# Handing out two small PSUM tiles in the order in which they come free

## The chip, the cores and the metric

The kernel runs on one core of a Trainium2 chip. The metric is the device time of one execution in microseconds (us): the median of several runs, lower is better. Before the change it was 32416.63 us, the median of 3 runs from 32408.93 to 32426.16.

## What is computed

Eight images of 56 x 56 pixels with 192 channels go through four layers, all in float32. Layer 0 sends half of the channels through three convolutions and the other half through a normalisation, a projection, a depthwise convolution and a selective scan in four directions; layers 1 and 2 are selective scans in four directions with a layer norm behind them; layer 3 is windowed attention (7 x 7 windows, shifted by 3, six heads) with an MLP. The scan is the bulk of the work:

```
def step(h, t):
    u_t, d_t, b_t, c_t = t
    h = jnp.exp(d_t[..., None] * A) * h + (d_t * u_t)[..., None] * b_t[:, :, None, :]
    return (h, jnp.einsum('bkdn,bkn->bkd', h, c_t))
...
delta = jax.nn.softplus(jnp.einsum('bkrl,kdr->bkdl', dts, dt_proj_w) + dt_proj_b[None, :, :, None])
...
yv = _ln(yv, out_norm_g, out_norm_b) * jax.nn.silu(z)
```

Here `h` has 16 states for each of 192 channels, `t` runs over 3136 pixels in each of four directions, and layer 0's norm works over the 192 channels of a pixel.

## The kernel before

**The scan steps.** `run` (line 766) walks 9216 steps: 8 images, three scan layers, four directions, four chunks of 784 pixels (`CK`), and within a chunk 24 steps of 128 rows (32 channels x 4 states). In each step ACT makes `exp(delta*A)` into a large PSUM tile `ps_x`, POOL makes `db` (delta*u times B), DVE runs the scan over 784 pixels, and DVE (three steps of four) or POOL (the fourth) multiplies by C into a buffer `hc`. Every third step PE adds up three `hc` buffers into the PSUM tile `ps_y` (`add_up`, line 992), and ACT copies the finished sums out (`merge`, line 1013). There are seven `hc` buffers, three `db` buffers and two `ps_x` tiles.

**Everything else is woven between the steps by hand.** Python generators record the other work: `prepare` (line 921: the softplus that makes delta for the next half chunk), `after` and `after_half` (lines 658 and 677: the norm behind each scan layer, and the projection to the next layer's B, C and dt), `ssm_front` and `conv_front` (layer 0's front and convolutions of the next image), and `attention_block` (line 1029: layer 3 of the image before). `run` lets the generators in three queues (`ahead`, `urgent`, `back`) advance piece by piece after each step. A `yield n` gives the turn back, for `n` steps if `n` is over 0. `together(2, ...)` (line 380) advances two generators in turn. The order in which the generators record their instructions is then the order on each engine: `in_order` (line 881) ties every instruction to the one recorded before it on its engine. What happens when on the chip is decided by these five queues and by semaphore waits.

**The small PSUM tiles.** Two tiles of 128 x 512 float32, called `ps_p`, serve all work outside the scan steps. A generator asks with `bank()` (line 351), which calls `all_banks(1)` (line 356). It yields until the count of free tiles, `self.banks`, is at least 1 and no queue of higher rank has asked in the last step. Then the count goes down and a tile is taken from the pool `self.psum` with tag `p` and two buffers: the pool gives its two buffers in turn. `free()` (line 365) puts the count up again. It is called when the last reader of the tile has been recorded, not when that reader has run. The pool adds the wait of the new user's first instruction for all that the previous user of the same buffer does.

**The users that matter below.** `ln_cm` (line 401) takes a tile, records two matmuls into it (the sums of the 192 channels, by a matrix of ones), two DVE instructions that subtract the mean (`act<-ps_p,act`), and frees it, without a yield between; then `to_norm` (line 413) takes a tile for the variance (`aux,ones`). `after` runs two halves of `after_half` in `together(2, ...)`. `softplus` (line 940) holds a tile from its matmul (`ps_p<-dts,dtw`) to its last DVE subtraction (`spe<-ps_p,spe`), over several yields; its two halves also run two at a time. The attention takes tiles for the query and key sums (`xb,wqkv`), their squared norms (`qksq,blk`), the scores (`biasl,ident` and `kn,qn`), the values (`wqkv,xw`), the transposed scores (`ident,s`), the weighted sums (`vt,pt`, read by DVE into `o`), and the transposed result (`ident,o`).

Matmuls are float32 and run as two passes each, transposes as one, so the profile shows more PE rows than the program has matmuls. Nearly all instructions pass through one helper that counts their load, so that their line in the profile is L109; they are told apart by the names of their tiles.

Of the kernel before, what the change touches and what calls it, by code (L numbers as in the profile page):

```python
# [31 lines left out]
F32 = mybir.dt.float32  # L32
# [6 lines left out]
C = 192  # L39
CH = 96  # L40
T = 448
# [7 lines left out]
HC = CK // 2  # L49
# [89 lines left out]
class Net:  # L139
    def __init__(self, ctx, tc, a, out):  # L140
        self.tc, self.nc, self.a, self.out = tc, tc.nc, a, out
        self.cp = ctx.enter_context(tc.tile_pool(name="const", bufs=1))
        self.dram = ctx.enter_context(tc.tile_pool(name="dram", bufs=1, space=bass.MemoryType.DRAM))
        self.dram2 = ctx.enter_context(
            tc.tile_pool(name="dram2", bufs=2, space=bass.MemoryType.DRAM)
        )
        self.psum = ctx.enter_context(tc.tile_pool(name="psum", bufs=2, space=bass.MemoryType.PSUM))
        self.psum1 = ctx.enter_context(tc.tile_pool(name="psum1", bufs=1, space=bass.MemoryType.PSUM))
        self.constants(ctx)
        self.wout = self.const("wout", [CH, 2, C])  # L150
        big = ctx.enter_context(tc.tile_pool(name="big", bufs=1))
        self.bufs = [big.tile([CH, 2, L], F32, name=f"act{n}") for n in range(2)]
        for n in (1, 2, 3, 4, 5):
            setattr(self, f"s{n}", ctx.enter_context(tc.tile_pool(name=f"s{n}", bufs=n)))
        self.s6 = ctx.enter_context(tc.tile_pool(name="s6", bufs=HCS))
        self.ranks = self.s1.tile([CH, CK], F32, name="dts")
        self.aux = [self.s1.tile([CH, 2, HC], F32, name=f"aux{n}") for n in range(2)]
        self.nc.gpsimd.memset(self.ranks, 1.0)
        self.done = set()
        self.nc = Engines(tc.nc)  # L160
        self.load = self.nc.load
        self.now, self.banks, self.rank, self.asked = 0, 2, 0, [-9] * 3
        self.ahead, self.urgent, self.back = deque(), deque(), deque()
        self.u0, self.sz, self.xl, self.u3, self.bcd = {}, {}, {}, {}, {}

    def ps(self, tag, p=128, n=512):
        if tag == "y":
            t = self.psum1.tile([128, 1024], F32, name="ps_y")
        else:
            w = 512 if tag == "p" else 1024  # L170
            t = self.psum.tile([128, w], F32, name=f"ps_{tag}", tag=tag)
        return t[:p, :n]
# [183 lines left out]
    def all_banks(self, n):  # L356
        rank = self.rank
        while self.banks < n or any(at >= self.now - 1 for at in self.asked[rank + 1 :]):
            self.asked[rank] = self.now
            yield 1  # L360
        self.asked[rank] = -9
        self.banks -= n
        return [self.psum.tile([128, 512], F32, name="ps_p", tag="p") for _ in range(n)]

    def free(self):

        self.banks += 1
# [33 lines left out]
    def ln_cm(self, x, n, sq):  # L401

        nc = self.nc
        p = (yield from self.bank())[:CH, :n]
        for c in range(2):
            nc.tensor.matmul(p, self.ones, x[:, c, :], start=c == 0, stop=c == 1)
        for c in range(2):
            nc.vector.scalar_tensor_tensor(x[:, c, :], p, -1.0 / C, x[:, c, :], ALU.mult, ALU.add)
        self.free()
        yield 1  # L410
        yield from self.to_norm(x, n, sq)

    def to_norm(self, x, n, sq):

        nc = self.nc
        nc.scalar.activation(sq, x, AF.Square)
        yield 1
        p = (yield from self.bank())[:CH, :n]
        for c in range(2):
            nc.tensor.matmul(p, self.ones, sq[:, c, :], start=c == 0, stop=c == 1)  # L420
        yield LAG
        nc.scalar.activation(p, p, AF.Ln, bias=self.eps[:CH], scale=1.0 / C)
        nc.scalar.activation(p, p, AF.Exp, scale=-0.5)
        yield 0
        for c in range(2):
            nc.vector.tensor_mul(x[:, c, :], p, x[:, c, :])
        self.free()
        yield 1
# [41 lines left out]
    def ssm_front(self, b):  # L470
# [3 lines left out]
        with tc.tile_pool(name="f1", bufs=1) as f1, tc.tile_pool(name="f2", bufs=2) as f2:  # L474
# [14 lines left out]
            def depthwise(r, c, u):  # L489
                p = (yield from self.bank())[:CH, :T]  # L490
                for tap in range(9):
                    dy, dx = tap // 3, tap % 3
                    nc.tensor.matmul(
                        p, diag[:, c, tap, :], pads[r % 3][:, c, dy : dy + ROWS, dx : dx + HW],
                        start=tap == 0, stop=tap == 8,
                    )
                    if tap % 3 == 2:
                        yield 1
                yield 1
                nc.scalar.activation(u[:, c, :], p, AF.Identity, bias=self.v("conv2d_b", c))  # L500
                self.free()
                yield 1

            def gate(xnt, r, e, sz):
                p = (yield from self.bank())[:CH, :T]
                nc.tensor.matmul(p, win[:, CH * e : CH * e + CH], xnt, start=True, stop=True)
                yield LAG
                if e < 2:
                    self.band(
                        [t[:, e] for t in pads], r,  # L510
                        lambda dst, rows: nc.scalar.copy(dst, grid(p)[:, rows, :]),
                    )
                else:
                    nc.scalar.copy(sz[:, e - 2, :], p)
                self.free()
                yield 1

            for r in range(NR + 1):
                sz = u = None
                if r < NR:  # L520
# [18 lines left out]
                    p = (yield from self.bank())[:CH, :T]  # L539
# [7 lines left out]
                    self.free()  # L547
# [17 lines left out]
    def conv_front(self, b):  # L565
# [3 lines left out]
        with tc.tile_pool(name="f1", bufs=1) as f1, tc.tile_pool(name="f2", bufs=2) as f2:  # L569
# [6 lines left out]
            def conv(w, pads, r):  # L576
                p = (yield from self.bank())[:CH, :T]
                for tap in range(9):
                    dy, dx = tap // 3, tap % 3
                    nc.tensor.matmul(  # L580
                        p, w[:, tap, :], pads[r % 3][:, dy : dy + ROWS, dx : dx + HW],
                        start=tap == 0, stop=tap == 8,
                    )
                    if tap % 3 == 2:
                        yield 1
                yield 1
                return p

            def first(r):
                tok = self.tokens(f2, b, r, "tokl", 0, CH)  # L590
                yield 2
                p = (yield from self.bank())[:CH, :T]
# [9 lines left out]
                self.free()  # L602
                yield 1

            def second(r):
                p = yield from conv(wc1, pad1, r)
# [5 lines left out]
                self.free()  # L612
                yield 1

            def third(r):
                p = yield from conv(wc2, pad2, r)
# [4 lines left out]
                self.free()  # L621
# [4 lines left out]
                def last(c):  # L626
                    p = (yield from self.bank())[:CH, :T]
# [3 lines left out]
                    self.free()  # L631
                    yield 1
                    p = (yield from self.bank())[:CH, :T]
# [7 lines left out]
                    self.free()  # L641
# [35 lines left out]
    def after_half(self, g, q):  # L677
# [22 lines left out]
        if l == 0:  # L700
# [6 lines left out]
            ps = [p[:CH, :HC] for p in (yield from self.all_banks(2))]  # L707
            for c in range(2):
                for j in range(2):
                    nc.tensor.matmul(  # L710
                        ps[c], self.wout[:, j, CH * c : CH * c + CH], y[:, j, :],
                        start=j == 0, stop=j == 1,
                    )
            yield LAG
            for c in range(2):
                nc.vector.tensor_add(y[:, c, :], ps[c], aux[:, c, :])
                self.free()
            yield 1

    def project(self, g, par, i):  # L720
# [7 lines left out]
        for q in range(2 * i, 2 * i + 2):  # L728
            p = (yield from self.bank())[:W, :HC]
# [8 lines left out]
            self.free()  # L738
# [182 lines left out]
    def prepare(self, U, h, start):  # L921
# [18 lines left out]
        def softplus(q):  # L940
            p = (yield from self.bank())[:CH, :HC]
# [17 lines left out]
            self.free()  # L959
# [99 lines left out]
    def attention(self, x, wi, bias, wqkv, wpr, q1, q2):  # L1059
# [15 lines left out]
        def normed(c, j, name):  # L1075
            p = (yield from self.bank())[:CH, :BT]
# [6 lines left out]
            self.free()  # L1083
# [3 lines left out]
            p = (yield from self.bank())[:CH, :BT]  # L1087
# [7 lines left out]
            if j:  # L1095
                nc.vector.tensor_mul(kn[:, c, :], p, t)
                self.free()
            else:
                nc.vector.tensor_mul(t, p, t)
                self.free()  # L1100
# [12 lines left out]
        def pair(w0):  # L1113
# [4 lines left out]
            for d in range(2):  # L1118
                w = w0 + d
                p = (yield from self.bank())[:WT, : HEADS * WT]  # L1120
# [21 lines left out]
                self.free()  # L1142
                yield 0
            p = (yield from self.bank())[:WT, : 2 * C].rearrange("n (d e) -> n d e", d=2)
# [11 lines left out]
            self.free()  # L1156
            pts = q2.tile([WT, 2, HEADS * WT], F32, name="pt")
            for d in range(2):
                p = (yield from self.bank())[:WT, : HEADS * WT]
# [6 lines left out]
                self.free()  # L1166
                yield 0
            yield 1
            p = (yield from self.bank())[:WT, : 2 * C].rearrange("n (d e) -> n d e", d=2)
# [12 lines left out]
            self.free()  # L1182
            yield 1
            p = (yield from self.bank())[:CH, : 4 * WT]
# [17 lines left out]
            self.free()  # L1202
# [5 lines left out]
        def project(c):  # L1208
            p = (yield from self.bank())[:CH, :BT]
# [8 lines left out]
            self.free()  # L1218
# [18 lines left out]
    def mlp(self, x, wi, b, f1b, wf1, q1, q2):  # L1237
# [5 lines left out]
        def expand(m):  # L1243
            p = (yield from self.bank())[:, :BT]
# [7 lines left out]
            self.free()  # L1252
# [9 lines left out]
        for c in range(2):  # L1262
            p = (yield from self.bank())[:CH, :BT]
# [8 lines left out]
            self.free()  # L1272
# [4 lines left out]
        def store(a):  # L1277
            n = min(2, WS - a) * HW
            p = (yield from self.bank())[:n, :C]
# [7 lines left out]
            self.free()  # L1287
# [143 lines left out]
```

## Time and profile before

| | |
|---|---|
| median of 3 runs | 32416.63 us |
| lowest and highest run | 32408.93 and 32426.16 us |
| the profiled execution, its own time | 32427.15 us |
| its span, first to last instruction | 32425.0 us |
| mean granted TensorE clock | 0.697 of full speed |
| DVE waits for PE work on `ps_p` before `o` | 467.2 us in 198 waits |
| DVE waits for POOL's `db` before a scan into `ps_x` | 757.9 us in 666 waits |
| DVE waits for POOL's `db` before a scan into `hc` | 39.7 us in 49 waits |
| DVE waits for PE work on `ps_y` before `hc` | 257.5 us in 124 waits |

PE is TensorE, PEld its weight loads, DVE VectorE, ACT ScalarE, POOL GpSimd, SP the engine that issues most DMAs. A group's row in the profile gives, after the shapes and the count, the busy time in us and the mean ns of one instruction, then the idle time of the engine just before the group's instructions and what ended most of it. The stretches of work repeat from layer to layer and image to image: over the 40 equal slices of the span DVE is 70 to 90% busy nearly throughout.

### The profile page before, as it was taken

Reading aid. Unit: us, or ns where it says so; the run is one execution under the profiler, and the core shown is the slowest. Engines: PE = TensorE matmul, PEld = TensorE weight load, DVE = VectorE, ACT = ScalarE, POOL = GpSimd, SP = SyncE. Lnnn points to the kernel's source line nnn. Section 1 sums busy time; section 2 is a strip of 40 time slices with the busy share of each in tenths; the row PEclk is TensorE's granted clock in tenths of the full one; section 3 lists DMA queues with packets and bytes.
Section 4 is the critical chain, followed back from the end, with each engine's and each line's share of the span. In section 5 each row is a group of like instructions: output and inputs, shape, how many; then the busy total and the mean of one; then the engine's idle time right before and its main releaser. Section 6 shows DMA issues by size and latency. Waiting matters only on the chain. (4 is left out here: it accounts for less than half of the span.)

```text
span 32425.0 us, 276524 instructions
## 1 busy us (share of the span) xinstructions
PE 20473.4 (63%) x77812; PEld 7417.8 (23%) x77812; DVE 25991.6 (80%) x22723; ACT 18456.6 (57%) x38862; POOL 24426.9 (75%) x14431
## 2 busy tenths in 40 slices
PE   4665466666666666666666666666666666666556
PEld 1221122222222222222222222222212222222123
DVE  2889887888888888888888888788887888888870
ACT  2555555565556655566555655556555665655553
POOL 2888877778777787778777787777877778777860
PEclk8776667667776777666776767767777667666666
DMA  2455544445444454444544455444544445444430
GB/s 57 116 124 115 115 113 106 111 103 124 111 108 104 109 126 109 108 105 113 121 105 111 106 117 117 107 107 108 118 116 106 107 108 120 108 110 106 110 88 13
DMA packets 1538509, 3473.09 MB, mean 107 GB/s; under 512 B 345563, under 2 KB 538164, under 8 KB 1536965
## 3 DMA queue, kind: packets, MB, share of 16 engines
q1 hardware_dynamic: 1533700, 3455.30, 46.3%
q8 instruction: 615, 10.08, 0.1%
q14 instruction: 930, 7.61, 0.1%
q10 hardware_dynamic: 2496, 0.09, 0.0%
q0 software_dynamic: 768, 0.01, 0.0%
HBM read 1457.23 MB, written 147.89 MB: 50 GB/s over the span
## 5 line engine op out<-in xcount | busy, mean ns | idle before, releaser
L109 POOL TENSOR_TENSOR db<-usp,bt 128x784 f32<-128x784 f32 x9216 | 16857.4, 1853 | 2672.5 <-DVE ps_x L109 1431.6
L109 DVE TENSOR_TENSOR_SCAN ps_x<-ps_x,state,db 128x784 f32<-128x784 f32 x5184 | 9563.7, 1845 | 1175.8 <-POOL db L109 565.4
L109 ACT ACTIVATE ps_x<-dsp,A 128x784 f32<-128x784 f32 x9216 | 8433.7, 916 | 2676.7 <-DVE hc L109 2476.5
L109 PE MATMUL ps_y<-hc,esum 128*32 128x392 f32 x36864 | 7205.9, 668 | 1598.6 <-POOL hc L109 1416.2
L109 DVE TENSOR_TENSOR hc<-ps_x,ct 128x784 f32<-128x784 f32 x6912 | 6738.8, 975 | 718.3 <-PE ps_y L109 106.4
L109 POOL TENSOR_TENSOR hc<-hc,ct 128x784 f32<-128x784 f32 x2304 | 4249.8, 1845 | 2876.2 <-ACT state L109 2370.9
L109 ACT COPY state<-ps_x 128x1 f32<-128x1 f32 x5184 | 812.8, 157 | 5513.7 <-DVE hc L109 5507.9
L109 DVE TENSOR_TENSOR_SCAN ps_x<-ps_x,db 128x784 f32<-128x784 f32 x1728 | 3083.8, 1785 | 592.6 <-ACT ps_x L109 265.4
L109 DVE TENSOR_TENSOR_SCAN hc<-ps_x,state,db 128x784 f32<-128x784 f32 x1728 | 3178.5, 1839 | 339.9 <-PE ps_y L109 133.0
L109 PEld LDWEIGHTS ps_y<-hc,esum 128*32 128x32 f32 x36864 | 1683.2, 134 | 6582.7 <-issue 3771.8
L109 PE MATMUL ps_p<-dts,dtw 13*96 13x392 f32 (+1 forms) x3072 | 1707.8, 679 | 1362.2 <-DMA dts<-bcd 954.6
L109 POOL TENSOR_TENSOR delta<-delta,spe 96x392 f32<-96x392 f32 x1536 | 1528.4, 1011 | 1292.9 <-DVE spe L109 1291.0
L109 PE MATMUL ps_y<-act,ident 96*96 96x392 f32 x2304 | 1657.7, 857 | 1105.8 <-ACT act L109 1005.3
L109 PE MATMUL ps_p<-act,wx 96*88 96x392 f32 (+1 forms) x1536 | 1042.1, 818 | 1119.6 <-DVE spe L109 794.1
L109 POOL TENSOR_TENSOR du<-delta,act 96x784 f32<-96x784 f32 x768 | 1564.5, 2037 | 60.2
L109 ACT ACTIVATE s<-ps_p,mx 49x49 f32<-49x49 f32 x3072 | 867.8, 296 | 512.2 <-DVE mx L109 511.5
L109 PEld LDWEIGHTS ps_p<-dts,dtw 13*96 13x96 f32 (+1 forms) x3072 | 538.8, 205 | 2469.2 <-issue 828.5
L109 PE MATMUL ps_p<-hid,wf 128*96 128x392 f32 x1536 | 739.5, 641 | 524.5 <-DMA wf<-wf2d 323.1
L109 ACT ACTIVATE delta<-ps_p 96x392 f32<-96x392 f32 x1536 | 736.3, 479 | 580.3 <-DMA dsp<-delta 283.4
L109 DVE SCALAR_TENSOR_TENSOR spe<-ps_p,spe 96x392 f32<-96x392 f32 x1536 | 818.7, 553 | 288.8 <-ACT ps_p L109 282.2
L109 DVE TENSOR_TENSOR_SCAN hc<-ps_x,db 128x784 f32<-128x784 f32 x576 | 1023.5, 1777 | 32.7 <-PE ps_y L109 18.2
L109 PE MATMUL ps_p<-xb,wqkv 96*96 96x392 f32 x1024 | 565.3, 711 | 751.2 <-DVE spe L109 429.3
(168 smaller groups left out, 25253.4 us busy)
## 6 DMA issues: line engine op xcount, KB each, us to landing
dsp<-delta SPq DMA_DIRECT2D x2304, 392.0 KB
usp<-du SPq DMA_DIRECT2D x2304, 392.0 KB
bt<-bcd SPq DMA_DIRECT2D x1536, 392.0 KB
ct<-bcd SPq DMA_DIRECT2D x1536, 392.0 KB
wf<-in_wf SPq DMA_DIRECT2D x128, 288.0 KB
wf<-wf2d SPq DMA_DIRECT2D x128, 288.0 KB
bcd<-bcx SPq DMA_DIRECT2D x256, 134.8 KB
szd<-sz SPq DMA_DIRECT2D x56, 336.0 KB
```

The costliest lines, as they stand in the source:

```text
L109: return call(out, *args, **k)
```

## The change

The two small tiles are allocated once, at the start, from the pool `psum1`, and kept in a deque `self.banks`. `all_banks` pops tiles from the left, `free(p)` appends the given tile at the right. So a tile is handed out again in the order in which the tiles were freed, as recorded, where before the pool gave its two buffers in turn. The condition under which a generator gets a tile (the number of free tiles, and who has asked) is the same. A tile freed while the other is still held is therefore the next one handed out. During the setup `ps("p")` rotates the deque. Everywhere else the generators keep the tile they got as `held` and give it back by name. The dependencies between two users of a tile now come from the accesses to one and the same tile, and no longer from the release of a pool's buffer.

```diff
+        self.banks = deque(self.psum1.tile([128, 512], F32, name=f"ps_p{n}") for n in range(2))
...
-        self.now, self.banks, self.rank, self.asked = 0, 2, 0, [-9] * 3
+        self.now, self.rank, self.asked = 0, 0, [-9] * 3
...
     def ps(self, tag, p=128, n=512):
         if tag == "y":
             t = self.psum1.tile([128, 1024], F32, name="ps_y")
+        elif tag == "p":
+            t = self.banks[0]
+            self.banks.rotate()
         else:
-            w = 512 if tag == "p" else 1024
-            t = self.psum.tile([128, w], F32, name=f"ps_{tag}", tag=tag)
+            t = self.psum.tile([128, 1024], F32, name=f"ps_{tag}", tag=tag)
         return t[:p, :n]
...
     def all_banks(self, n):
         rank = self.rank
-        while self.banks < n or any(at >= self.now - 1 for at in self.asked[rank + 1 :]):
+        while len(self.banks) < n or any(at >= self.now - 1 for at in self.asked[rank + 1 :]):
             self.asked[rank] = self.now
             yield 1
         self.asked[rank] = -9
-        self.banks -= n
-        return [self.psum.tile([128, 512], F32, name="ps_p", tag="p") for _ in range(n)]
-
-    def free(self):
-
-        self.banks += 1
+        return [self.banks.popleft() for _ in range(n)]
+
+    def free(self, p):
+
+        self.banks.append(p)
...
     def ln_cm(self, x, n, sq):
 
         nc = self.nc
-        p = (yield from self.bank())[:CH, :n]
+        held = yield from self.bank()
+        p = held[:CH, :n]
         for c in range(2):
             nc.tensor.matmul(p, self.ones, x[:, c, :], start=c == 0, stop=c == 1)
         for c in range(2):
             nc.vector.scalar_tensor_tensor(x[:, c, :], p, -1.0 / C, x[:, c, :], ALU.mult, ALU.add)
-        self.free()
+        self.free(held)
         yield 1
```

All other users are edited as `ln_cm` is.

## The prediction

> **What bounds the kernel now.** I read the page's totals first, then the waits of each engine, then single stretches of the timeline.
>
> ```profile
> span 32425.0 us, 276524 instructions
> PE 20473.4 (63%) x77812; PEld 7417.8 (23%) x77812; DVE 25991.6 (80%) x22723; ACT 18456.6 (57%) x38862; POOL 24426.9 (75%) x14431
> L109 POOL TENSOR_TENSOR db<-usp,bt 128x784 f32<-128x784 f32 x9216 | 16857.4, 1853 | 2672.5 <-DVE ps_x L109 1431.6
> L109 DVE TENSOR_TENSOR_SCAN ps_x<-ps_x,state,db 128x784 f32<-128x784 f32 x5184 | 9563.7, 1845 | 1175.8 <-POOL db L109 565.4
> ```
>
> No engine is full. DVE is nearest: 80%, with POOL at 75%, and each waits for the other in the scan steps. PE, the only engine that takes a small bank, is busy 63%. A PE wait costs time only if a DVE or POOL instruction then starts late.
>
> ```profile
> PE ps_p L109 <- DVE spe L109: 3963.3, 673, 17.7
> PE ps_p L109 <- DVE act L109: 358.2, 168, 5.4
> DVE mx L109 <- PE ps_p L109: 981.2, 452, 5.9
> DVE act L109 <- PE ps_p L109: 346.9, 224, 13.5
> ```
>
> In these lines (who waited for whom: us in total, times, longest) the first is large and tempting: a bank whose last reader is the softplus's subtraction. But a softplus pair holds both banks, so whoever is next must wait for that subtraction under either rule. The last line is the reverse: DVE's centring in `ln_cm` waits for PE's sums. There the change bites.
>
> **What the change alters.** Both programs issue the same instructions in the same order on every engine: `all_banks` yields at the same counts as before, so no task moves, no DMA is added, and SP's queue has not even a different wait. Only bank numbers and waits differ; the setup's hand-outs stay in turn. Of 6551 hand-outs of a small tile, 591 get a bank whose previous user is another than before; 342 times the bank is the one handed out just before. For each of the 591 I compared, in the trace of before, when the old previous user's readers ended with when the new one's did. For 501 both ended before PE was free for the matmul: price 0, hidden by PE's own queue. 17 would start earlier, by 8.2 us together. 73 would start later.
>
> *The 30 costly ones* are the second halves in `ln_cm`. That function takes a bank, issues its matmuls and both DVE readers, and frees the bank without a yield. If a background task holds the other bank, the second half now gets the very bank that the first has just given up; in turn, it got the other one, whose reader, though recorded later, had long run on ACT. One such place, around 6841 us:
>
> ```profile
> 6840.20 2.87 PE L109 MATMUL ps_p<-act,ones 96*96 96x392 f32 x8
> 6841.80 1.04 DVE L109 SCALAR_TENSOR_TENSOR act<-ps_p,act 96x392 f32<-96x392 f32 x2 [3.80 <-PE ps_p L109]
> 6842.91 0.87 PE L109 MATMUL ps_p<-qksq,blk 96*96 96x392 f32 x2
> 6843.11 1.04 DVE L109 SCALAR_TENSOR_TENSOR act<-ps_p,act 96x392 f32<-96x392 f32 x2 [0.28 <-PE ps_p L109]
> 6844.07 0.56 DVE L109 TENSOR_SCALAR ps_p<-ps_p 96x392 f32<-96x392 f32 x1
> 6846.41 1.84 POOL L109 TENSOR_TENSOR db<-usp,bt 128x784 f32<-128x784 f32 x1 [4.10 <-DVE ps_x L109]
> ```
>
> (Start us, duration, engine, operation, count, and in brackets the idle time and who ended it.) The eight passes are two halves; the second starts after half of 2.87 us, at 6841.6, while DVE reads the first half, so DVE idles 0.28 us between halves. After the change the second half starts when DVE has read the first: 6841.80 + 1.04 = 6842.84, plus the 0.07 us that the 6842.91 matmul took after that same reader. Its four passes take 1.47 us (6841.60 to 6843.07), DVE follows 0.04 later: 6842.91 + 1.47 + 0.04 = 6844.42 instead of 6843.11, so 1.31 us lost. Thirty times: **39.3 us of DVE**. Behind the waiting matmul on PE stand the query's `qksq` sums and then the `ps_y` matmuls; behind the late DVE reader stand a scan and, through it, POOL's `db` (4.10 us idle for DVE in the last line) and ACT.
>
> *Seven `qksq` matmuls* of the attention follow such a half and get the same bank a third time: 6844.42 + 1.04 + 0.07 + 0.87 + 0.04 = 6846.44 against 6844.07, 2.37 us, of which 1.31 is counted: 1.06 x 7 = **7.4 us**. *Six `biasl` matmuls* now wait for the DVE reader of a `vt,pt` tile. In the place at 6966 us the matmul started at 6966.03; that reader ran 6966.25 to 6966.80, plus 0.07, so 0.84 us late, and DVE's `mx` waits for it: 0.84 x 6 = **5.0 us**. *Four single places* have a reader that follows at 0.04 to 0.5 us: 4 x 1.1 = about **4 us**.
>
> *The other 26* (9 softplus halves, late by 0.5 to 1.9 us; 7 `ident,o` transposes; 6 `aux,ones` sums; four more) make PE late by 28 us together, but their readers on ACT start 1.5 to 5.2 us after the matmul's end, because ACT is busy before them. Price 0; without that cover, 28 us.
>
> *The 17 gains* are the hand-outs just after a swapped one, as the `biasl` matmul that waited 0.81 us for the second `ln_cm` half. PE issues in order and the late matmul stands right ahead of it, so I take 0; bound 8.2 us.
>
> *Wait instructions.* Separate waits change by +156 on DVE, +223 on ACT, -292 on PE. Those waits are long satisfied by the trace's times. The rows of such an instruction in the last chain take 0.03 to 0.04 us, so 6 us on DVE at most, 0 if the sequencer runs ahead, as DVE's rows without a gap suggest. I take 0.
>
> Sum on DVE: 39.3 + 7.4 + 5.0 + 4 = 56 us. How much of it reaches the end?
>
> ```profile
> 6846.00:6866.00 20.00, 13.76 (x47) 4.84 (x48) 17.49 (x20) 17.35 (x36) 11.86 (x7) 0.83 0.41 83
> 6740.00:6860.00 120.00, 76.40 (x242) 25.09 (x244) 97.60 (x91) 70.56 (x124) 86.72 (x52) 0.69 0.44 98
> ```
>
> (The stretch, its length, then busy time of PE, PEld, DVE, ACT, POOL, the granted clock, DMA share, GB/s.) Right after such a place DVE is busy 17.49 of 20 us, 87%, and what gaps it has are ended by PE and ACT work on `ps_p` that the same delay moves. Only in waits for POOL could DVE catch up; over the whole run DVE's waits for POOL's `db` are 757.9 + 39.7 us of 32425.0 - 25991.6 = 6433 us idle. So most passes: 80% of 56, **+45 us**. Bounds: all losses absorbed and the gains kept, -8; everything exposed, 56 + 28 + 6 = +90.
>
> One rule of the Trainium skill speaks against the change (Perfetto Trace Analysis, section Matmuls under Optimizing Tensor Performance): independent matmul groups should rotate through PSUM banks, so that the reading-out of one overlaps the next group's matmuls. The overlap it means is the row at 6840.20 above. Taken as a rule for all 342 repeated hand-outs it would cost 342 x 1.31 = 448 us, an estimate by that page; the trace leaves 73, since elsewhere the reader is done before PE arrives.
>
> **The rivals.** *Absorbed:* PE is 63% and DVE 80% busy, and the losses come in places some 80 us apart, so DVE could make up each 1.3 us out of its idle fifth; then 32417 us, give or take 15. Against it: DVE runs back to back after these places. Within the same band as my forecast.
>
> *Slower by over 0.2%:* the covers fail together. The late matmul holds PE's queue, so the `ps_y` sums behind it come late, the `hc` buffers are freed late, and DVE's multiply waits as well (DVE already waits 257.5 us for `ps_y`). If the 28 us lose their cover and all passes, 32417 + 90 = 32507 us. It decides from 65 us on, that is if all 56 pass and a third of the 28 comes too.
>
> *Faster:* the order of freeing lets PE off part of the 3963.3 us behind `DVE spe`. If waits were spread evenly over hand-outs, 591/6551, 9%, or 357 us of PE would be touched; a fifth of it reaching the end would be -71 us, 32345 us. Against it: the place-by-place comparison finds 8.2 us.
>
> **How the numbers follow.** Forecast: same band, +45 us; the profiled execution (32427.15 us, span 32425.0) lies 10.5 us above the median of the runs, so on the median, 32416.63 + 45 = **32462 us**. About 0.2%, 65 us, is what a measurement of this kernel can tell from no change. Chances: mostly passed on, +25 to +65 us, 0.46; absorbed, -15 to +25, 0.21; over +65, 0.27; faster by over 65, 0.06. That gives faster 0.06, same 0.67, slower 0.27. The range takes the bounds -8 and +90 and some 15 us of the runs' own spread (they span 17): 32395 to 32525. The likeliest case alone is 32442 to 32482.
>
> **What would show it.** Right: the gap before the second centring pair grows from 0.28 to about 1.6 us at 30 places, more waits under DVE `act` <- PE `ps_p` (+40 us) and PE `ps_p` <- DVE `act` (+35 or more), `DVE spe` within 5% of 3963, busy times of all engines unchanged within 0.2%. Wrong: the DVE waits grow and the span doesn't (absorbed), `DVE spe` falls by hundreds of us, or `ps_y` waits on DVE grow beyond 300 us. Other busy times, through a different granted clock, would also break it, since I keep every duration.

## The result, and the profile after

The changed kernel takes 32494.44 us, the median of nine runs from 32463.42 to 32510.76; before, nine runs on the same chip have a median of 32416.63. The ratio is 1.0024, with an interval from 1.0014 to 1.0034: slower by 78 us, between 45 and 110. The forecast was +45 us, and its range, 32395 to 32525, holds the result; the narrower stretch given for the likeliest case, 32442 to 32482, does not. The ratio lies just past the 0.2% that was set as the bound of "no change", with an interval on both sides of it. A second set of runs of the same kernel gave 1.0023 [1.0014, 1.0032], so the loss is real; its size is known to about 30 us either way.

The profiled execution is the shortest of the nine (32463.42 us), and the one shown of before was 10 us above its median. The two spans therefore differ by only 36.6 us. Below, the traces tell where the time goes, and the medians tell how much.

From the page of the changed kernel, the totals and the two largest groups:

```profile
span 32461.6 us, 276612 instructions
...
PE 20422.7 (63%) x77812; PEld 7393.2 (23%) x77812; DVE 25990.3 (80%) x22723; ACT 18448.1 (57%) x38862; POOL 24453.1 (75%) x14431
...
L109 POOL TENSOR_TENSOR db<-usp,bt 128x784 f32<-128x784 f32 x9216 | 16885.5, 1854 | 2704.3 <-DVE ps_x L109 1445.1
L109 DVE TENSOR_TENSOR_SCAN ps_x<-ps_x,state,db 128x784 f32<-128x784 f32 x5184 | 9562.0, 1845 | 1175.4 <-POOL db L109 554.8
```

The counts of the working engines are the same and their busy times moved by 0.25% at most, the weight loads by 0.33% (the granted clock was 0.701 against 0.697; in the second set, at 0.696, PE is busy 20494.8 us, on the other side of the 20473.4 of before). The scan still takes 1845 ns, and `db` 1854 ns. No work was added, so all of the loss is waiting. The waits of the changed kernel (who waited for whom: us in total, times, longest):

```profile
PE ps_p L109 <- DVE spe L109: 4054.7, 696, 17.9
...
DVE mx L109 <- PE ps_p L109: 976.5, 445, 5.4
...
PE ps_p L109 <- DVE act L109: 421.5, 217, 5.3
DVE act L109 <- PE ps_p L109: 402.8, 232, 13.5
...
DVE hc L109 <- PE ps_y L109: 258.1, 132, 5.7
```

PE's waits behind DVE's `act` rose by 63 us (from 358.2), DVE's waits for PE before `act` by 56 us (from 346.9): the two halves of one loop, PE waiting for the reader and the next reader waiting for PE. `mx` and the `ps_y` wait before `hc` hardly moved. PE's largest wait rose by 91 us; whether that costs anything is settled by the run that changes the 30 places and moves nothing.

The place that the prediction showed around 6841 us, in the timeline of the changed kernel (start, duration, engine, operation, count, and in brackets the idle time and who ended it):

```profile
6846.59 1.56 PE L109 MATMUL ps_p<-act,ones 96*96 96x392 f32 x4
...
6848.18 1.03 DVE L109 SCALAR_TENSOR_TENSOR act<-ps_p,act 96x392 f32<-96x392 f32 x2 [1.68 <-PE ps_p L109]
...
6849.27 1.56 PE L109 MATMUL ps_p<-act,ones 96*96 96x392 f32 x4 [1.13 <-DVE act L109]
...
6850.87 1.03 DVE L109 SCALAR_TENSOR_TENSOR act<-ps_p,act 96x392 f32<-96x392 f32 x2 [1.65 <-PE ps_p L109]
...
6851.96 1.56 PE L109 MATMUL ps_p<-qksq,blk 96*96 96x392 f32 x4 [1.13 <-DVE act L109]
...
6852.89 0.57 DVE L109 TENSOR_SCALAR ps_p<-ps_p 96x392 f32<-96x392 f32 x1 [0.99 <-PE ps_p L109]
```

The eight passes that stood in one row are now two rows of four. The second four start 1.13 us after the first four, when DVE has read the tile, and DVE's gap before its second centring pair is 1.65 us where it was 0.28: 1.37 us lost. The `qksq` matmul takes the same tile a third time, and DVE's gap behind it is 0.99 us more. The waits between the halves and behind the third use are what the prediction drew.

Both programs record the same instructions in the same order, so the two traces can be laid against each other instruction by instruction. Here a place is the moment at which the second half's matmul starts in the trace of before. Taking for each place how far DVE's next instruction has shifted against the trace of before, relative to 3 us ahead of the place, the mean over the 30 places is 1.52 us at 1.6 us after it, 2.12 (give or take 0.19) at 3 us, 2.26 at 20 us and 1.91 (0.22) at 80 us. The delay doesn't shrink to anything near zero within 80 us, which is about as close as the next place ever comes.

| second halves of `ln_cm` | places | DVE's shift after 3 us |
|---|---|---|
| now on the first half's tile, before not | 30 | 2.12 us |
| on the first half's tile already before | 32 | 0.0 us |
| on two tiles in both programs | 25 | 0.1 us |

The other nine of the 96 second halves have other DVE work between the halves. Thirty times 2.12 is 64 us. The middle row is a correction too: it has 32 pairs that shared a tile before the change, which a pool that gave its two buffers strictly in turn would not have produced. The tile names in the recorded programs show that the pool gave the same buffer twice running 244 times (after the change 342), and that 250 hand-outs have another previous user than before, not 591.

### The profile page after: what moved, and what is told of

The parts are those of the page before. It is cut to its first block, busy times and chain, and to the rows that moved or that the text cites. A ratio compares the mean times of both kernels' runs of the same rounds, so it can differ in the third digit from the quotient of the medians.

```text
span 32461.6 us, 276612 instructions
## 1 busy us (share of the span) xinstructions
PE 20422.7 (63%) x77812; PEld 7393.2 (23%) x77812; DVE 25990.3 (80%) x22723; ACT 18448.1 (57%) x38862; POOL 24453.1 (75%) x14431
## 5 line engine op out<-in xcount | busy, mean ns | idle before, releaser
L109 POOL TENSOR_TENSOR db<-usp,bt 128x784 f32<-128x784 f32 x9216 | 16885.5, 1854 | 2704.3 <-DVE ps_x L109 1445.1
L109 DVE TENSOR_TENSOR_SCAN ps_x<-ps_x,state,db 128x784 f32<-128x784 f32 x5184 | 9562.0, 1845 | 1175.4 <-POOL db L109 554.8
```

What stands on the lines that cost most here:

```text
L109: return call(out, *args, **k)
```

## The experiments

In all of them the computation is whole; only waits, tiles or the recorded order are changed. Ratios are to the kernel before, run on the same chip; they go by all runs of both kernels (they lie within 0.0001 of the quotient of the means), so that the quotient of two medians can differ in the fourth place.

**The loss put into the kernel before.** Here the pool stays, and the second half of a pair reuses the first half's tile where the other one is held and nothing was handed out between:

```diff
-    def ln_cm(self, x, n, sq):
+    def ln_cm(self, x, n, sq, again):
...
-        p = (yield from self.bank())[:CH, :n]
+        if again and self.banks == 1 and self.latest[1] == self.taken:
+            self.banks -= 1
+            p = self.latest[0]
+        else:
+            p = (yield from self.bank())[:CH, :n]
+            self.latest = p, self.taken
```

> The kernel before, with one change: the second half of ln_cm uses the first half's tile again where the other tile is held, so that 30 second halves wait for the first half's readers as in the changed kernel (in 32 other places the pool does so already). Theory (the 30 repeats make the loss): the pair costs DVE 1.37 us each as in the trace of the changed kernel, 30 x 1.37 = 41 us, and up to 63 us where the query's sums follow: 32457 to 32480 us, ratio 1.0012 to 1.0020. Rival (the loss lies in the other hand-outs or in the waits of tiles that are kept): within 15 us of 32417.

Measured: 32440.05 us, 1.0014 [1.0005, 1.0022]; the kernel before took 32402.65 us on that chip, so the expectation's ratio is met and its microseconds, which were counted from 32417, are not. The waits of this kernel:

```profile
DVE act L109 <- PE ps_p L109: 406.8, 237, 15.3
```

60 us more than before in that line, about as much as in the changed kernel, with the pool still handing out everything else. In the trace the 30 places shift by 1.77 us each (0.13 either way) at 3 us and 1.85 at 80 us: 53 us, within the interval of 16 to 71. That is less than the 64 of the changed kernel because less follows a place: between 1.6 and 3 us after it the shift grows by 0.12 us here and by 0.60 there. This part of the change alone makes the kernel slower, and the delay is kept.

**The loss made larger.** In the changed kernel, the second half takes the tile that was freed last. Of the 25 pairs that still had two tiles, 22 then get one as well; three keep two:

```diff
+        if again and len(self.banks) == 2:
+            self.banks.rotate()
         held = yield from self.bank()
```

> The changed kernel, with the second half of ln_cm always given the tile that was freed last: the 25 pairs that used two tiles now use one as well. Theory: 25 x 1.37 = 34 us more than the changed kernel, 32494 + 34 = 32528 us; waits under DVE act <- PE ps_p up by about 34 us on 403. Rival (such delays are absorbed by DVE's idle fifth): 32494, waits up all the same.

Measured: 32524.12 us, 1.0041 [1.0027, 1.0055].

```profile
DVE act L109 <- PE ps_p L109: 432.4, 229, 13.5
```

The line rises by another 29.6 us. The 25 pairs shift by 1.34 us each in the trace, 34 us in sum, while the 30 old places have 2.30. In the 22 that repeat, the gap ahead of the second half's reader grows by 1.37 or 1.44 us, from 0.28 to 1.65 or from 1.58 to 3.02. The time alone would not show this: its interval overlaps that of the change (1.0014 to 1.0034).

**Two attempts to take the loss out that moved the recorded order.** First, the second half waits one scan step if only one tile is free:

```diff
+        if again and len(self.banks) == 1:
+            yield 1
         held = yield from self.bank()
```

> The changed kernel, with the second half of ln_cm recorded a step later where only one tile is free: a scan step's DVE work then lies between the two halves. Theory (the 30 repeats make the loss): 40 to 63 us less than the changed kernel, 32431 to 32454 us. Rival (loss elsewhere): 32494, plus or minus 15 for the moved order.

Measured: 32600.65 us, 1.0062 [1.0049, 1.0075], slower than the change itself. Two lines of its waits:

```profile
PE ps_p L109 <- DVE spe L109: 4150.3, 699, 17.8
...
POOL db L109 <- DVE ps_x L109: 1639.8, 928, 27.8
```

DVE's wait before `act` did fall, to 319.0 us, below the kernel before. But POOL's wait for DVE's scan rose from 1445.1 to 1639.8: the `yield` moves thousands of instructions to other places in the queues (by the rows of the trace 3083 on DVE, 9625 on ACT, 13228 on PE). The theory's number failed, and the run says nothing about the 30 places.

A second attempt lets the background generator that holds the other tile advance until it gives it back, and takes that one:

```diff
+        for _ in range(6 * again):
+            if len(self.banks) == 1 and self.piece(self.back, True):
+                if len(self.banks) == 2:
+                    self.banks.rotate()
         held = yield from self.bank()
```

> The changed kernel; where only one tile is free when the second half of ln_cm begins, the background task that holds the other is first advanced until it gives it back, and the second half takes that one. So the repeats in ln_cm go, with little else moved (684 of the 22723 DVE places). Theory (the repeats make the whole loss, 64 to 72 us in the traces, and the 32 pairs that shared a tile in the kernel before as well go too, 1.4 us each): 0.9990 to 1.0005 on the kernel before. Rival (a further cost of kept tiles or of the order of freeing, or of moved work as when the second half waited a step): 1.0015 or more.

Measured: 32461.23 us, 1.0019 [1.0010, 1.0028], outside what the theory expected and in the range of its rival.

```profile
DVE ps_x L109 <- POOL db L109: 815.4, 703, 5.1
...
DVE act L109 <- PE ps_p L109: 347.0, 205, 17.0
```

The local loss is gone: the wait before `act` is back at the 346.9 us of before, and at the 30 places DVE is shifted by -0.03 us after 10 us. Still the kernel is no faster, with DVE's waits for `db` at 815.4 us against 746.7 in the changed kernel. 684 DVE instructions moved. What that movement costs in detail was not taken apart; an undo that changes the recorded order is no clean undo, and the runs with two pools, below, were built to move nothing.

**The readers put a step behind.** In `ln_cm`, the generator gives the turn back between the matmuls and their DVE readers (`LAG` is 1 step), first in the changed kernel, then in the kernel before:

```diff
             nc.tensor.matmul(p, self.ones, x[:, c, :], start=c == 0, stop=c == 1)
+        yield LAG
         for c in range(2):
```

> The changed kernel, with the readers in ln_cm recorded a step after the matmuls, as the other users of a small tile do: DVE no longer waits for the sums, 402.8 us in 232 waits in the changed kernel. Theory (DVE sets the pace, four fifths of a DVE delay reach the end): 0.8 x 403 = 320 us less, 32170 us, below both kernels. Rival (each tile is held a step longer, and what asks for it next comes late): no gain, 32450 to 32550 us.

> The kernel before, with the readers in ln_cm recorded a step after the matmuls. With the kept tiles this gave 0.9953. Theory (only the halves of ln_cm tell the two ways of handing out apart, and here they no longer do): 0.9953, plus or minus 0.0008. Rival (kept tiles or the order of freeing cost some 30 us elsewhere): 0.9940 to 0.9945.

Measured: 32243.55 us, 0.9953 [0.9941, 0.9965] on the changed kernel; 32195.49 us, 0.9935 [0.9923, 0.9947] on the kernel before. The waits of the first:

```profile
PE ps_p L109 <- DVE act L109: 493.0, 210, 9.5
...
DVE act L109 <- PE ps_p L109: 77.8, 77, 11.7
```

and of the second:

```profile
PE ps_p L109 <- DVE act L109: 391.1, 175, 9.5
...
DVE act L109 <- PE ps_p L109: 79.7, 77, 11.7
```

DVE no longer waits for the sums it has just ordered: some 325 us fewer in that line (from 402.8), and about 230 us of it reach the end (0.9953 against 1.0024), some 70%. The gain is under the 320 us that were expected of the first run; the second one's number was expected to equal the first and was 0.18% lower, on the side of the rival, which laid 30 us on kept tiles or on the order of freeing. The run with two pools, below, finds no cost of kept tiles. The line that differs is PE's wait for `act`, 493.0 against 391.1. With the changed hand-out the tile that `ln_cm` has just used is given out again, and its readers are now a step late, which would explain it. The two programs have the same instructions in the same order, and of the 61 us between their traces most stands ahead of DVE's readers in the attention (24 us before `mx`, 16 before `ps_p`, 11 before `o`), which wait for PE; but the explanation was not tried by itself.

**Is it the kept tiles or the order?** The tiles are allocated once, as in the change, but each hand-out takes the tile that the pool chose in the kernel before, wherever it is free as recorded (a table of 6551 bits); 122 hand-outs then differ from before, among them the 30.

```diff
-        return [self.banks.popleft() for _ in range(n)]
+        return [self.chosen() for _ in range(n)]
...
+    def chosen(self):
+        t = self.pair[int(POOL[self.given])]
+        self.given += 1
+        if t not in self.banks:
+            return self.banks.popleft()
+        self.banks.remove(t)
+        return t
```

> The changed kernel's two kept tiles, but each hand-out takes the tile that the pool gave in the kernel before, wherever that tile is free as recorded; elsewhere the other. 122 of the 6551 hand-outs then have another previous user than before (the 30 second halves of ln_cm and what follows them, mostly), against 250 in the changed kernel. Theory (the 30 places): like the changed kernel less little, 1.0015 to 1.0022 on before. Rival A (the order of freeing at the other 128 costs): 1.0013 or less, near the kernel with the shared tile. Rival B (kept tiles cost by their extra waits, 156 on DVE and 223 on ACT): like the changed kernel, above 1.0022.

Measured: 32499.51 us, 1.0029 [1.0018, 1.0039], as slow as the change. So the order of freeing, outside the places where it forces a repeat, costs nothing that these intervals show. The number itself lies above the theory's 1.0022, where the rival of costly kept tiles stood, so that question stayed open. The opposite run keeps the changed hand-out order but takes a new tile each time, from one of two pools with one buffer each:

```diff
-        return [self.banks.popleft() for _ in range(n)]
+        return [self.take(self.banks.popleft()) for _ in range(n)]
+
+    def take(self, n):
+        p = self.pools[n].tile([128, 512], F32, name="ps_p", tag="p")
+        self.owner[id(p)] = n, p
+        return p
```

> The changed kernel's order of hand-outs, with a new tile from one of two pools of one buffer each in place of the two kept tiles: the same banks in the same order, with a pool's release. Theory (the order of hand-outs is all): like the changed kernel, 1.0018 to 1.0028 on the kernel before. Rival (kept tiles cost some 30 us): 1.0008 to 1.0015.

Measured: 32473.72 us, 1.0025 [1.0015, 1.0034].

```profile
DVE act L109 <- PE ps_p L109: 401.1, 231, 13.5
```

The same time and the same line as the change (402.8), and outside the 1.0008 to 1.0015 of the rival. Allocating once or each time makes no difference that the intervals show; what counts is which tile is given.

**The 30 places, with nothing moved.** The kernel of the last run, but at the 30 second halves the tile that is taken is the one still held as recorded, whose reader has run by then on the chip. Every instruction keeps its place on its engine. With the 30 repeats go 30 later ones that hung on them, among them the third uses by `qksq`.

```diff
-        held = yield from self.bank()
+        self.seconds += again
+        turn = again and self.seconds in OTHER
+        if turn:
+            assert len(self.banks) == 1
+            held = self.take(1 - self.banks[0])
+        else:
+            held = yield from self.bank()
...
-        self.free(held)
+        if not turn:
+            self.free(held)
```

> As the kernel with the two pools, but in the 30 second halves of ln_cm that repeated a tile the other tile is taken, although its holder has not given it back as recorded; so the pool in the kernel before did. No instruction moves. Theory (the 30 places are all): 64 to 72 us less than with the two pools alone, 0.9998 to 1.0006 on the kernel before. Rival (the other hand-outs cost some 30 us as well): 1.0007 to 1.0015.

Measured: 32399.21 us, against 32399.19 for the kernel before on that chip: 1.0004 [0.9995, 1.0013]. The loss is gone, as far as the interval tells. Its waits:

```profile
PE ps_p L109 <- DVE spe L109: 4080.5, 695, 18.3
...
PE ps_p L109 <- DVE act L109: 386.8, 184, 5.4
...
DVE act L109 <- PE ps_p L109: 348.1, 222, 13.5
```

and the place around 6841 us in its timeline, DVE alone:

```profile
6829.44 1.03 DVE L109 SCALAR_TENSOR_TENSOR act<-ps_p,act 96x392 f32<-96x392 f32 x2 [3.83 <-PE ps_p L109]
6830.76 1.04 DVE L109 SCALAR_TENSOR_TENSOR act<-ps_p,act 96x392 f32<-96x392 f32 x2 [0.28 <-PE ps_p L109]
6831.71 0.56 DVE L109 TENSOR_SCALAR ps_p<-ps_p 96x392 f32<-96x392 f32 x1
```

The gap is 0.28 us again, and over the 30 places DVE's shift against before is 0.04 us (0.11 either way). PE waits 117 us longer behind `DVE spe` than in the kernel before, and the time is the same: that wait has cover. Of the 119 hand-outs that became repeats by the change, 59 are still in this kernel, the ten of the softplus among them; they cost nothing that the interval can show. The run doesn't part the 30 places from the 30 repeats that hang on them; that the second halves alone cost time is shown by the run that put them into the kernel before.

**The same delay of readers everywhere.** What the runs with late readers showed for `ln_cm` holds for three more places where DVE reads a tile as soon as it is recorded: the `qksq` sums, the scores before `mx`, the weighted sums before `o`. Four `yield LAG`, in the kernel before and in the changed one:

```diff
             nc.tensor.matmul(p, self.blk, sq, start=True, stop=True)
+            yield LAG
...
+                yield LAG
                 nc.vector.reduce_max(
```

> The kernel before, with the readers recorded a step late in ln_cm and also in the attention, where DVE waits for PE right behind the matmuls (mx 981 us, o 467, ps_p 428 in the kernel before). If DVE's waits set the pace everywhere: four fifths of a further 1876 us, down to 30800 us. Rival (the tiles are held longer and the softplus is late, as when the second half waited a step): from 32250 up, and above 32417 if that outweighs all.

> The changed kernel, with the readers recorded a step late in ln_cm and in the attention, as in the fastest kernel so far, which has the pool (0.9686). Theory (handing out matters only where a tile comes back at once while PE waits; with readers a step late, repeats are mended by the work between, but a tile is held longer, so that the next user more often gets the one just freed): 0.9686 to 0.9705. Rival (handing out in the order of freeing helps once tiles are scarce): below 0.9680.

Measured: 31381.99 us, 0.9686 [0.9673, 0.9700] on the kernel before, and 31400.88 us, 0.9693 [0.9680, 0.9706] on the changed one. The first is the fastest kernel of this study. Its waits:

```profile
DVE hc L109 <- PE ps_y L109: 560.6, 236, 9.4
...
DVE ps_p L109 <- PE ps_p L109: 269.7, 49, 26.8
...
DVE mx L109 <- PE ps_p L109: 259.8, 161, 4.9
...
DVE o L109 <- PE ps_p L109: 167.1, 36, 9.3
...
DVE act L109 <- PE ps_p L109: 56.8, 58, 5.1
```

The second line of these was, in the kernel before:

```profile
DVE ps_p L109 <- PE ps_p L109: 428.2, 102, 27.3
```

The last four stood at 428.2, 981.2, 467.2 and 346.9 us before, 2223.5 in sum, and are 753.4 now: 1470 us of DVE's waits gone. The span is 1047 us shorter, 71% of that. Some is given back in the first line, which was 257.5: DVE now waits 303 us more for the `ps_y` sums. The expectation took four fifths of a further 1876 us, down to 30800. That was too much: of the 1876 only 1180 went, and the `ps_y` line is part of why no more of them reached the end. With the readers late, the hand-out order makes no difference that these runs can tell: the two intervals overlap almost wholly.

## Why the prediction was right, and where it was off

*The mechanism was right and is shown.* The change bites at 30 second halves of `ln_cm`, which get the tile that the first half has just given up. Put into the kernel before, those 30 repeats alone make it slower (1.0014 [1.0005, 1.0022]); taken out of the changed program, with 30 later repeats that hung on them and without moving an instruction, the loss is gone (1.0004 [0.9995, 1.0013]). The `ps_y` wait (258.1 us, bound 300) and `DVE spe` (+2.3%, bound 5%) stayed inside what the prediction named, and the gap (0.28 to 1.65 us, "about 1.6"), DVE's wait (+56, named +40) and PE's (+63, named 35 or more) went as it said. PE's busy time was 0.25% off where 0.2% was named, and the weight loads' 0.33%; PE's is on the other side in the second set's profile.

*The term of the sum that was mis-sized most, as far as the traces tell, is the pass to the end, "80% of 56".* The trace shows 2.12 us at 3 us after a place and 1.91 at 80 us, equal within their errors; taken alone this would not rule out a fifth made up (1.70). Over the traces of five kernels that have the 30 repeats (the change, its second set, and the runs with the pool's choice, with two pools and with more repeats) the shift is 2.26 at 3 us, 2.46 at 40 us and 2.12 at 80 us, and the last is 0.14 below the first (0.21 either way), where a fifth would be 0.45. DVE is idle for a fifth of the time, but in the wait lines that idle time is waiting for PE, ACT and POOL, and delayed DVE work would delay those too; that reason was not tried by itself.

*The loss of a place was a little larger than the sum had it.* The second half cost 1.37 us and not 1.31; the third use by `qksq` 1.08 and not 1.06; `biasl`, at seven places right behind a second half, only about 0.4 and not 0.84. With all that follows a place, the shift is 64 us over the 30 places, where the prediction had 56. The median of +78 us, interval 45 to 110, contains 64. The difference between the two was not taken apart.

*The count of changed hand-outs was wrong and cost nothing.* "591" came from a pool that gives its buffers strictly in turn. It doesn't; 250 hand-outs change. The price was formed from what the new reader's end does to the matmul at each place, and there the 30 stood out under either count. By the same fault the text spoke of a pool in turn at places that already shared a tile.

*What was costed at nothing was near nothing.* At the ten softplus halves with a new repeat DVE's shift after 3 us is between -0.12 and 0.55 us, 1 us in sum. The added wait instructions: `mx` has 129 instructions with one wait more, and the median gap ahead of them is 1853 ns against 1851. The 59 other repeats and PE's longer waits behind `spe` cost nothing that shows in the run that moved nothing.

*The rivals.* "Absorbed" falls: the loss is there in the changed kernel, and again where it was put in alone. "Faster" falls, since no part of the 3963.3 us behind `spe` was released (4054.7 now). The slower rival named the right side of the bound with the wrong mechanism: its covers did not fail, `ps_y` waits moved by 0.6 us, and with the softplus halves among them left in, the run that moved nothing is as fast as before. If the loss is past 0.2%, it is because the first sum was larger and came through nearly whole.

*The rule on rotating PSUM banks* (the Trainium skill, Perfetto Trace Analysis, section Matmuls under Optimizing Tensor Performance) points the right way in the 30 places, where it names the overlap that was lost. By repeats it doesn't hold here: 119 of the hand-outs became new repeats, 30 of them make DVE's gap longer by 1.37 us or more, and a program with 59 of the others left in is as fast as before.

## What to carry to other kernels

Which of two tiles came free first in the recorded program is not which came free first on the chip: where each engine's order is fixed, compare at each changed hand-out when the old and the new previous reader end, and price only where the new one ends later than the engine is ready. A microsecond lost on the busiest engine, at a place where it waits for the others, came through nearly whole here, although that engine was idle for a fifth of the time; of the waits that the late readers took out, some 70% came through. And a DVE reader recorded directly behind its matmul waits for it with everything behind it: recording it one step later was worth 3.1% here, more than any choice of tiles.

## What the hardware showed that was not expected

More waits per instruction cost nothing that shows. With kept tiles 129 of the 512 `mx` instructions on DVE carry one wait more, and the median idle time ahead of them is 1853 against 1851 ns; 146 of the 768 copies of `ps_y` on ACT carry one more too, and the median one starts without a gap in both programs. The prediction had kept up to 6 us for the waits on DVE.
